# Graph attention, layers 1 to 3: exponential factors in the table rows in place of raw scores

## The chip, the core and the metric

The program runs on one core of one Trainium2 chip. The metric is the device time of a run in microseconds (us); the time before is the median of three runs, 3008.34 us (2991.2 to 3010.58). Five engines of the core do the work: TensorE (PE, whose weight loads the profile lists as PEld), VectorE (DVE), ScalarE (ACT), GpSimd (POOL) and SyncE (SP). Each runs its own instructions in order; semaphores tie them to each other, and DMA queues move data between the device's memory (DRAM) and the two memories on chip, SBUF and PSUM.

## The reference

Four graph-attention layers work on one graph of 3327 nodes and on features x (3327 x 512, float32). Each layer normalises x, applies ReLU, lets each node average over its neighbours with attention weights, and adds the result to x. The heads are 8, 4, 1 and 8; layers 0 and 1 count a node as its own neighbour, and layers 1 and 2 apply ELU.

```python
def layer(x, l):                                  # l = 0 .. 3, H = 8, 4, 1, 8
    h = relu(layernorm(x))
    v = (h @ W[l]).reshape(n, H, 512 // H)
    s = einsum("nhd,hd->nh", v, a_own[l])         # score of the node that averages
    d = einsum("nhd,hd->nh", v, a_other[l])       # score of the neighbour
    e = leaky_relu(s[:, None, :] + d[None, :, :], 0.2)
    e = where(neighbours[:, :, None], e, -inf)
    alpha = softmax(e, axis=1)
    y = einsum("ijh,jhd->ihd", alpha, v).reshape(n, 512)
    return x + (elu(y) if l in (1, 2) else y)
```

A neighbour's weight before the division by the sum is exp(leaky(s + d)), with leaky(z) = max(z, 0.2 z). Since the exponential of a sum is a product, it is also exp(0.2 s) exp(0.2 d) max(exp(0.8 s) exp(0.8 d), 1). The first factor depends only on the node that averages, so the division by the sum of the weights removes it.

## The kernel before

**Prologue.** The nodes are padded to 3328, 26 tiles of 128. The first 313 us read the adjacency matrix, take from each row a list of its neighbours' numbers, sort the rows by the length of their lists (CAPS holds the longest list of each tile, 36 down to 11) and project the features for layer 0 into a table in DRAM. Only then does `tile_gat_lists` begin, which all that follows is about.

**The table.** Between layers, each node's row lies in a DRAM table (`tabs`, two of them in turn). A row has ROW = 528 numbers in two halves of 264: 256 projected features and 8 score columns. Behind the first half are the node's own scores s, behind the second its scores d as a neighbour. Layer 0 has a table of its own (`tabx`).

**A tile with lists (class Tile).** A step is a group of four list entries of one tile: 133 steps in layer 0, then 118, 72 and 105. `fetch` is called seven steps ahead: POOL issues one indirect DMA for each entry (L834), which brings 128 table rows, one for each partition, into g; in layers 1 to 3 the node's own row (entry 0) comes through SP (L865). `scored` runs one step ahead of the products. It copies s out of the own row at a tile's first step (L885), adds s to the d columns of g (z, L887), applies the leaky slope (L889), both on VectorE, and lets ACT write the exponential into pw (L890). pw is a PSUM bank that holds the weights of a whole tile; in layer 2 it lies in SBUF instead. `group` then multiplies the gathered features by the weights on VectorE (m, L918, four operations of 512 columns; a tile's first goes to the accumulator itself), and PE adds m to the accumulator ("bank") with an identity as the weights (L923). Buffers: seven g, three m, two accumulators. In layer 2, with its one head, VectorE accumulates by itself (L909, L911).

**Behind a tile.** `finish` and `ends` spread the rest over the next steps: the sum of the weights and its reciprocal (L929 to L931), the division (L937, L941), ELU with two ACT operations (neg L947, ex L949) and one on VectorE (L955), the sum into x (L957, L961), the centred row xn and its squares on ACT (L969, L972), the reciprocal root on VectorE (ve L977, then L434 to L440), the transposes (L450), the ReLU (hT, L457), the projection for the next layer (L468), the scaling by ACT into v (L475), and SP's write of v to the table (L995). In PSUM, the projection's result pv has a bank for each half of the row.

**Tiles done densely.** The tiles with the longest lists go against all 3328 rows under a mask: one tile in layer 1, nine in layer 2, three in layer 3 (DENSE = [0, 1, 9, 3]). Layers 1 and 3 use `Several`: 52 units u, the 26 tiles of rows twice, half of the heads each time. For a unit SP loads half of the table rows and a mask (L1250, L1251; three buffers each). In the first 26 units ACT makes exp(0.8 d) and exp(0.2 d) of all heads (L1261, L1262). Then ACT forms r = relu(exp(0.8 s) exp(0.8 d) - 1) for each head (L1267) and the features times exp(0.2 d) (L1278, L1279; two buffers); VectorE masks r + 1 (L1283), PE multiplies (L1301, into "whole"). exp(0.8 s) of the dense tiles, one node for each column, is made once (L1241, L1243). `Wholes` does the same for layer 2, three passes of three tiles over 26 row tiles j: the loads of ve and the mask (L1105, L1107; four and three buffers), in the first pass exp(d), exp(0.2 d) and its negative (L1115 to L1117), r (L1119), the mask (em, L1126), the products (L1153), and partial sums of the weights on POOL and VectorE.

**The order.** The order of PE, VectorE, ACT and POOL is written out by hand. `later(step, place, piece)` files a piece under a step and one of three places, and a loop issues each step as: fetches, the "first" pieces, `scored` of the next step, the "scored" pieces, `group` of this step, the "last" pieces. The dense work's masked tile and product are "first" pieces, and its r, features and next loads "scored" pieces. So they stand in the engines' queues between the pieces of the list tiles:

```python
do("first")
if s + 1 < len(steps):
    steps[s + 1][0].scored(steps[s + 1][1])
do("scored")
if 0 <= s < len(steps):
    tl, i = steps[s]
    tl.group(i)
    if i == len(tl.k0) - 1:
        tl.finish(s)
do("last")
```

The waits follow from the buffers that instructions share; in this program a wait that concerns a PSUM buffer covers its whole bank.

Of the kernel before, what the change touches and what calls it, by code (L numbers as in the profile page):

```python
# [18 lines left out]
P = 128  # L19
# [504 lines left out]
def tile_gat_stack(ctx: ExitStack, tc: tile.TileContext, x, adj, adjT, ws, avs, out):  # L524
# [32 lines left out]
    spare = late.tile([P, 2, slots.parts[1].columns], F32, name="spare")  # L557


    with ExitStack() as c1:  # L560
# [49 lines left out]
        def late_constants():  # L610
# [5 lines left out]
            for t in tabs:  # L616
                nc.sync.dma_start(t[NP:NP + 1, :], pad[:, :ROW])
# [173 lines left out]
    with cond.Else():  # L791
        tile_gat_lists(tc, x, adj, ws, avs, out, ident, half, slots, L, low, spare, tabx, tabs)
# [3 lines left out]
def tile_gat_lists(ctx: ExitStack, tc: tile.TileContext, x, adj, ws, avs, out, ident, half, slots, L, low, spare, tabx, tabs):  # L796
# [48 lines left out]
    class Tile:  # L845
# [29 lines left out]
        def scored(self, i):  # L875
# [4 lines left out]
            if i == 0:  # L880
                self.po = pools["o"].tile([P, BANK], F32, name="bank")
                pw = next(scores)
                K = CAPS[t]
                self.wt, self.s = pw[:, :K * 8].rearrange("p (k h) -> p k h", h=8), pw[:, K * 8:K * 8 + H]
                nc.vector.tensor_copy(self.s, g[:, n, F:F + H] if self.l == 0 else g[:, 0, F // 2:F // 2 + H])  # L885
# [5 lines left out]
            if self.l == 0:  # L891
                ranks = n - (i == 0)
                nc.scalar.activation(slots(t, max(k0, 1), count=ranks), g[:, :ranks, F // 2], AF.Copy)
                if i == 0:
                    nc.scalar.activation(xs[self.t], g[:, n, :F], AF.Copy)

# [95 lines left out]
        def rows(self):  # L992
            if self.W is not None:
                v = scaled(nc, self.pv, self.rstd, work)
                nc.sync.dma_start(tabs[(self.l + 1) % 2][self.t * P:(self.t + 1) * P, :], v)  # L995
# [86 lines left out]
    class Wholes:  # L1082


        def __init__(self, l, W):
            self.l, self.tiles = l, [Whole(l, t, W) for t in range(ND)]
            self.s = pools["e"].tile([P, ND], F32, name="s", bufs=1)
            for t in range(ND):
                nc.sync.dma_start(self.s[:, t:t + 1], tabs[l % 2][t * P:(t + 1) * P, F // 2:F // 2 + 1])
            self.b, self.c, self.mc = [pools["e"].tile([P, NT], F32, name=n, bufs=1) for n in ("b", "c", "mc")]  # L1090
# [4 lines left out]
        def targets(self, p):  # L1095

            pa = pools["t"].tile([P, F // P, P], F32, name="pt")
            for q in range(3):
                nc.tensor.matmul(pa[:, q, :], self.s[:, 3 * p + q:3 * p + q + 1].to_broadcast([P, P]), ident,
                                 start=True, stop=True)  # L1100
            nc.scalar.activation(self.a[p], pa[:, :3, :], AF.Exp, scale=1.0 - SLOPE)
# [7 lines left out]
        def weights(self, p, j):  # L1109
            if p == ND // 3:  # L1110
                return
            b, c, mc = [t[:, j:j + 1] for t in (self.b, self.c, self.mc)]
            if p == 0:
                d = self.v[p, j][:, ROW - 8:ROW - 7]
                nc.scalar.activation(b, d, AF.Exp)  # L1115
                nc.scalar.activation(c, d, AF.Exp, scale=SLOPE)
# [4 lines left out]
        def masked(self, p, j):  # L1121
# [4 lines left out]
            nc.vector.scalar_tensor_tensor(self.e[p, j], self.r.pop((p, j)), self.c[:, j:j + 1],  # L1126
# [43 lines left out]
        def place(self, n):  # L1170

            per = n // (ND // 3)
            for p in range(ND // 3):
                s0 = p * per
                later(s0 - 4 if p else -1, "first", lambda p=p: self.targets(p))
                for j in range(NT):
                    s = s0 + j * (per - 2) // NT
                    later(max(s - 3, -1), "first", lambda p=p, j=j: self.load(p, j))
# [27 lines left out]
    class Several:  # L1206
# [3 lines left out]
        def __init__(self, l, n, W):  # L1210
# [10 lines left out]
            self.c, self.b = [room(NT * Q * 2).rearrange("p (j h) -> p j h", j=NT) for _ in range(2)]  # L1221

# [3 lines left out]
            self.s = room(n * 8).rearrange("p (t h) -> p t h", h=8)  # L1226
            for t in range(n):
                nc.sync.dma_start(self.s[:, t, :self.H],
                                  tabs[l % 2][t * P:(t + 1) * P, F // 2:F // 2 + self.H])
            self.per = BANK // DV - (self.H == 8)  # L1230

        def begin(self):
# [20 lines left out]
        def weights(self, u):  # L1253
# [215 lines left out]
```

## Time and profile before

The profiled execution spanned 2971.7 us.

| | us |
|---|---|
| median of three runs | 3008.34 |
| the three runs | 3008.34, 2991.2, 3010.58 |
| span of the profiled execution | 2971.7 |
| PE busy (share of the span) | 2211.9 (74%) |
| DVE busy | 1923.1 (65%) |
| POOL busy | 1731.4 (58%) |
| ACT busy | 934.6 (31%) |

The table says that no engine is busy throughout. The page's costliest groups of instructions name the work: each line gives the source line, engine, operation, output and inputs with their shapes and the count; then busy time and the mean ns of one; then the engine's idle time just before them, and what ended most of it.

```profile
L923 PE MATMUL bank<-m,ident 128*128 128x512 f32 x2414 | 1232.2, 659 | 335.9 <-DVE m L918 197.3
L918 DVE TENSOR_TENSOR m<-g,pw 128x512 f32<-128x512 f32 x1207 | 752.5, 682 | 384.1 <-ACT pw L890 209.2
L890 ACT ACTIVATE pw<-z 128x32 f32<-128x32 f32 (+4 forms) x356 | 67.8, 191 | 850.7 <-DVE z L889 484.2
```

The three are the chain of one step read backwards: PE adds m, VectorE makes m from g and the weights, ACT makes the weights. The last column is the reading to learn: before the multiplications VectorE had stood idle for 384.1 us in all, of which 209.2 us ended when ACT delivered pw; and ACT's own work there takes 191 ns each time. A wait of this kind need not mean that the exponential is slow. ACT may have come to it late because its queue held something else. The same column is given for a single instruction in the chronological lists below, in brackets at the end of a line.

### The profile page before, as it was taken

The numbers are of one execution on the slowest core, as the hardware profiler recorded it, in microseconds if no ns is written. First come the engines' busy times: TensorE is split into PE (matmuls) and PEld (weight loads), VectorE is DVE, ScalarE is ACT, GpSimd is POOL, SyncE is SP. The second block draws the span as 40 slices with busy tenths as digits, with TensorE's granted clock in tenths as the row PEclk, the third lists the DMA queues.
The fourth block names the chain that finished last, engine by engine and source line by source line (L and its number), as shares of the span: only waits on it lengthen the run. The fifth ranks groups of instructions, "written<-read, shape, count | busy, mean of one in ns | idle before, by whom it ended". The sixth has DMA issues, their size and how long they took to land.

```text
span 2971.7 us, 27155 instructions
## 1 busy us (share of the span) xinstructions
PE 2211.9 (74%) x7082; PEld 1246.1 (42%) x7082; DVE 1923.1 (65%) x4968; ACT 934.6 (31%) x2502; POOL 1731.4 (58%) x1717
## 2 busy tenths in 40 slices
PE   4777677776777764767777877588696688878887
PEld 2564233343433332434444444244354454545443
DVE  7987666655565533656665665598888366666665
ACT  5872122322221111322222322244333333323330
POOL 7885455565566635544556562676664556555653
PEclk9988888888898887988888898799898898989888
DMA  6885576786676756755667673787785566656663
GB/s 230 325 291 161 165 228 200 211 254 207 195 225 197 199 130 200 200 157 174 187 190 210 179 209 92 234 255 240 241 246 153 168 193 204 185 170 198 195 189 111
DMA packets 260731, 594.21 MB, mean 200 GB/s; under 512 B 103699, under 2 KB 121107, under 8 KB 256214
## 3 DMA queue, kind: packets, MB, share of 16 engines
q0 software_dynamic: 124368, 432.13, 49.8%
q1 hardware_dynamic: 132454, 153.45, 16.4%
q10 hardware_dynamic: 3744, 6.82, 0.7%
q8 instruction: 57, 0.93, 0.1%
q14 instruction: 108, 0.88, 0.1%
HBM read 542.60 MB, written 49.65 MB: 199 GB/s over the span
## 4 chain that ended last, share of the span: by engine, by line
PE 24%; DVE 18%; issue 14%; another core or an unknown queue 8%; ACT 5%; POOL 3%; DMA 2%; SPq 0%; DVEq 0%; POOLq 0%; ACTq 0%
PE bank L923 16%; DVE m L918 6%; PE pv L468 4%; PE whole L1301 3%; DVE bank L911 3%; POOL g L834 3%; ACT r L1267 1%; DVE z L889 1%; DVE z L887 1%; DVE x L961 1%; PE whole L1153 1%; DMA g<-tab,idxb 1%; DVE em L1126 1%; DVE q L438 1%
## 5 line engine op out<-in xcount | busy, mean ns | idle before, releaser
L923 PE MATMUL bank<-m,ident 128*128 128x512 f32 x2414 | 1232.2, 659 | 335.9 <-DVE m L918 197.3
L918 DVE TENSOR_TENSOR m<-g,pw 128x512 f32<-128x512 f32 x1207 | 752.5, 682 | 384.1 <-ACT pw L890 209.2
L834 POOL DMA_INDIRECT g<-tab,idxb x712 | 678.8, 953 | 482.0 <-issue 197.1
L923 PEld LDWEIGHTS bank<-m,ident 128*128 128x128 f32 x2414 | 488.8, 211 | 942.1 <-issue 582.4
L468 PE MATMUL pv<-w,hT 128*128 128x264 f32 x1664 | 434.9, 416 | 87.8 <-ACT hT L457 61.8
L834 POOL DMA_INDIRECT g<-tabx,twiceb x342 | 324.8, 950 | 230.7 <-issue 147.7
L834 POOL DMA_INDIRECT g<-tab,idxa x297 | 283.7, 955 | 248.4 <-issue 83.9
L468 PEld LDWEIGHTS pv<-w,hT 128*128 128x128 f32 x1664 | 334.1, 205 | 190.3 <-ACT hT L457 68.7
L890 ACT ACTIVATE pw<-z 128x32 f32<-128x32 f32 (+4 forms) x356 | 67.8, 191 | 850.7 <-DVE z L889 484.2
L1153 PE MATMUL whole<-ve,em 128*128 128x512 f32 x468 | 229.4, 642 | 54.1 <-issue 22.9
L1301 PE MATMUL whole<-L,room 128*128 128x130 f32 x1248 | 173.3, 290 | 59.9 <-issue 59.5
L1301 PEld LDWEIGHTS whole<-L,room 128*128 128x128 f32 x1248 | 164.7, 202 | 91.4 <-issue 89.7
L694 POOL TENSOR_TENSOR key<-a,keys 128x3328 int32<-128x3328 int32 (+1 forms) x29 | 189.3, 6530 | 16.3 <-DVE cand L703 11.8
L911 DVE SCALAR_TENSOR_TENSOR bank<-g,L,bank 128x512 f32<-128x512 f32 x243 | 183.3, 754 | 11.1 <-remote 2.0
L1153 PEld LDWEIGHTS whole<-ve,em 128*128 128x128 f32 x468 | 94.0, 206 | 167.4 <-issue 124.5
L834 POOL DMA_INDIRECT g<-tabx,twicea x99 | 94.7, 956 | 104.1 <-issue 51.1
L450 PE MATMUL pt<-ident,xn 128*128 128x128 f32 x416 | 70.8, 298 | 104.7 <-ACT xn L969 60.8
L703 DVE MAX8 cand<-key 128x8 f32<-128x208 int32 x416 | 144.3, 365 | 0.1
L475 ACT ACTIVATE v<-pv,rstd 128x528 f32<-128x528 f32 x78 | 54.2, 694 | 274.4 <-remote 126.5
L1267 ACT ACTIVATE r<-low,L 128x384 f32<-128x384 f32 x208 | 121.2, 583 | 16.9 <-remote 9.5
L918 DVE TENSOR_TENSOR bank<-g,pw 128x512 f32<-128x512 f32 x74 | 51.5, 696 | 100.7 <-ACT pw L890 69.2
L450 PEld LDWEIGHTS pt<-ident,xn 128*128 128x128 f32 x416 | 54.7, 153 | 144.4 <-ACT xn L969 69.1
(180 smaller groups left out, 2195.7 us busy)
## 6 DMA issues: line engine op xcount, KB each, us to landing
a<-in_adj SPq DMA_DIRECT2D x25, 1664.0 KB
tab<-v SPq DMA_DIRECT2D x78, 264.0 KB
ve<-tab SPq DMA_DIRECT2D x78, 264.0 KB
g<-tab SPq DMA_DIRECT2D x65, 264.0 KB
tabx<-vx SPq DMA_DIRECT2D x26, 528.0 KB
g<-tab,idxb POOLq DMA_INDIRECT x712
low<-tab SPq DMA_DIRECT2D x52, 132.0 KB
spare<-tab SPq DMA_DIRECT2D x52, 132.0 KB
```

Source lines behind the costliest of these rows:

```text
L450: nc.tensor.transpose(pt[:, k, :], xn[:, k * P:(k + 1) * P], ident)
L468: nc.tensor.matmul(pv[:, s, :HF + 8], hT[:, k, :], W.w[:, k, s, :], start=(k == 0), stop=(k == KC - 1))
L694: nc.gpsimd.tensor_tensor(key[:, c:c + quarter], a[:, c:c + quarter], keys[:, c:c + quarter], OP.mult)
L703: nc.vector.max(cand[:, g * 8:(g + 1) * 8], key[:, g * SEG:(g + 1) * SEG])
L834: nc.gpsimd.indirect_dma_start(out=out_, out_offset=None, in_=table, in_offset=bass.IndirectOffsetOnAxis(ap=which, axis=0))
L890: nc.scalar.activation(self.wt[:, k0:k0 + n, :H], z, AF.Exp)
L911: nc.vector.scalar_tensor_tensor(acc, v, w, acc, OP.mult, OP.add)
L918: nc.vector.tensor_tensor(out_.rearrange("p (s h d) -> p s h d", s=2, d=D), v.rearrange("p s (h d) -> p s h d", d=D), wt[:, k0 + q, :H].re ...
L923: nc.tensor.matmul(self.po, ident, m[:, q, :], start=False, stop=(k0 + q == K - 1), skip_group_check=True)
L1153: nc.tensor.matmul(tl.po.rearrange("p (s m) -> p s m", s=2), e[:, q * P:(q + 1) * P], v.rearrange("p (s m) -> p s m", s=2)[:, :, :F // 2], ...
L1267: nc.scalar.activation(self.r[:, h, :], self.a[:, g, :], AF.Relu, bias=-1.0, scale=self.b[:, j, g:g + 1])
L1301: nc.tensor.matmul(dst, e[:, h, q * P:(q + 1) * P], mov, start=False, stop=(j == NT - 1), skip_group_check=True)
```

## The change

In layers 1 to 3 the table rows carry exponentials of the scores, and the weights come from products and maxima on VectorE.

- `rows` adds four small ACT operations per tile, between the scaling (L475) and the table write (L995): a copy of d, scaled, out of pv; exp(0.8 s) into a tile `mine` that stays in SBUF, one column per tile and head; and two exponentials of d, which take the place of raw scores in v. With several heads these are exp(0.8 d) and exp(0.2 d), half of the heads behind each half of the row; with one head exp(d) and exp(0.2 d).
- `scored` of layers 1 to 3 calls `factored` and ends there: with several heads z = exp(0.8 s) exp(0.8 d), then max(z, 1) exp(0.2 d) straight into pw; with one head a single operation. The copy of s, the addition, the leaky slope and ACT's exponential leave these layers. Layer 0 keeps them.
- The dense parts no longer load s nor make exponentials of d; they read the factors from the rows loaded for the products. The exponential that made exp(0.8 s) for the targets becomes a copy.
- In layer 2 the first row tile of the second and third pass is loaded a step earlier.
- The tables' padding row becomes zeros. `mine` is handed through as an argument (not shown).

```diff
--- before
+++ after
@@ -555,6 +555,7 @@
...
     spare = late.tile([P, 2, slots.parts[1].columns], F32, name="spare")
+    mine = [late.tile([P, NT, n], F32, name=f"mine{n}") for n in (1, 8)]
...
@@ -614,7 +615,7 @@
...
             for t in tabs:
-                nc.sync.dma_start(t[NP:NP + 1, :], pad[:, :ROW])
+                nc.sync.dma_start(t[NP:NP + 1, :], pad[:, ROW:])
...
@@ -882,7 +883,11 @@
...
                 self.wt, self.s = pw[:, :K * 8].rearrange("p (k h) -> p k h", h=8), pw[:, K * 8:K * 8 + H]
-                nc.vector.tensor_copy(self.s, g[:, n, F:F + H] if self.l == 0 else g[:, 0, F // 2:F // 2 + H])
+                if self.l == 0:
+                    nc.vector.tensor_copy(self.s, g[:, n, F:F + H])
+            if self.l > 0:
+                self.factored(g, k0, n)
+                return
             z = small.tile([P, GROUP, 8], F32, name="z")[:, :n, :H]
...
@@ -893,6 +898,23 @@
...
                     nc.scalar.activation(xs[self.t], g[:, n, :F], AF.Copy)
+        def factored(self, g, k0, n):
+            H = HEADS[self.l]
+            a = mine[self.l % 2][:, self.t, :H]
+            w = self.wt[:, k0:k0 + n, :H]
+            if H == 1:
+                c0 = ROW - 8
+                nc.vector.scalar_tensor_tensor(w, g[:, :n, c0:c0 + 1], a, g[:, :n, c0 + 1:c0 + 2], OP.mult, OP.max)
+                return
+            Q, c0 = H // 2, F // 2
+            rows = g[:, :n, :].rearrange("p k (s m) -> p k s m", s=2)
+            z = small.tile([P, GROUP, 8], F32, name="z")[:, :n, :H].rearrange("p k (s h) -> p k s h", s=2)
+            nc.vector.tensor_tensor(z, rows[:, :, :, c0:c0 + Q],
+                                    a.rearrange("p (s h) -> p s h", s=2).unsqueeze(1).to_broadcast([P, n, 2, Q]), OP.mult)
+            nc.vector.scalar_tensor_tensor(w.rearrange("p k (s h) -> p k s h", s=2), z, 1.0,
+                                           rows[:, :, :, c0 + Q:c0 + 2 * Q], OP.max, OP.mult)
         def group(self, i):
...
@@ -992,6 +1014,19 @@
         def rows(self):
...
                 v = scaled(nc, self.pv, self.rstd, work)
+                H = HEADS[self.l + 1]
+                d = small.tile([P, 8], F32, name="d")[:, :H]
+                nc.scalar.activation(d, self.pv[:, 1, F // 2:F // 2 + H], AF.Copy, scale=self.rstd)
+                nc.scalar.activation(mine[(self.l + 1) % 2][:, self.t, :H], v[:, F // 2:F // 2 + H], AF.Exp,
+                                     scale=1.0 - SLOPE)
+                if H == 1:
+                    parts = [v[:, ROW - 8 + i:ROW - 7 + i] for i in range(2)]
+                else:
+                    Q, d = H // 2, d.rearrange("p (s h) -> p s h", s=2)
+                    halves = v.rearrange("p (s m) -> p s m", s=2)
+                    parts = [halves[:, :, F // 2 + i * Q:F // 2 + (i + 1) * Q] for i in range(2)]
+                nc.scalar.activation(parts[0], d, AF.Exp, scale=1.0 if H == 1 else 1.0 - SLOPE)
+                nc.scalar.activation(parts[1], d, AF.Exp, scale=SLOPE)
                 nc.sync.dma_start(tabs[(self.l + 1) % 2][self.t * P:(self.t + 1) * P, :], v)
         def ends(self, s):
...
@@ -1084,10 +1119,7 @@
         def __init__(self, l, W):
             self.l, self.tiles = l, [Whole(l, t, W) for t in range(ND)]
-            self.s = pools["e"].tile([P, ND], F32, name="s", bufs=1)
-            for t in range(ND):
-                nc.sync.dma_start(self.s[:, t:t + 1], tabs[l % 2][t * P:(t + 1) * P, F // 2:F // 2 + 1])
-            self.b, self.c, self.mc = [pools["e"].tile([P, NT], F32, name=n, bufs=1) for n in ("b", "c", "mc")]
+            self.mc = pools["e"].tile([P, NT], F32, name="mc", bufs=1)
...
@@ -1096,9 +1128,9 @@
...
             for q in range(3):
-                nc.tensor.matmul(pa[:, q, :], self.s[:, 3 * p + q:3 * p + q + 1].to_broadcast([P, P]), ident,
+                nc.tensor.matmul(pa[:, q, :], mine[self.l % 2][:, 3 * p + q, 0:1].to_broadcast([P, P]), ident,
                                  start=True, stop=True)
-            nc.scalar.activation(self.a[p], pa[:, :3, :], AF.Exp, scale=1.0 - SLOPE)
+            nc.scalar.activation(self.a[p], pa[:, :3, :], AF.Copy)
         def load(self, p, j):
...
@@ -1109,11 +1141,9 @@
         def weights(self, p, j):
...
                 return
-            b, c, mc = [t[:, j:j + 1] for t in (self.b, self.c, self.mc)]
+            b, c = [self.v[p, j][:, ROW - 8 + i:ROW - 7 + i] for i in range(2)]
+            mc = self.mc[:, j:j + 1]
             if p == 0:
-                d = self.v[p, j][:, ROW - 8:ROW - 7]
-                nc.scalar.activation(b, d, AF.Exp)
-                nc.scalar.activation(c, d, AF.Exp, scale=SLOPE)
                 nc.scalar.activation(mc, c, AF.Copy, scale=-1.0)
...
@@ -1123,7 +1153,7 @@
...
             self.e[p, j] = self.two[:, j % 2, :]
-            nc.vector.scalar_tensor_tensor(self.e[p, j], self.r.pop((p, j)), self.c[:, j:j + 1],
+            nc.vector.scalar_tensor_tensor(self.e[p, j], self.r.pop((p, j)), self.v[p, j][:, ROW - 7:ROW - 6],
                                            self.mk.pop((p, j)), OP.add, OP.mult)
...
@@ -1175,7 +1205,8 @@
...
                     s = s0 + j * (per - 2) // NT
-                    later(max(s - 3, -1), "first", lambda p=p, j=j: self.load(p, j))
+                    early = s0 - 4 if p and j == 0 else s - 3
+                    later(max(early, -1), "first", lambda p=p, j=j: self.load(p, j))
...
@@ -1218,15 +1249,9 @@
...
             self.e = [room(Q * n * P).rearrange("p (h c) -> p h c", h=Q) for _ in range(2)]
-            self.c, self.b = [room(NT * Q * 2).rearrange("p (j h) -> p j h", j=NT) for _ in range(2)]
             self.vs = [room((Q + (self.H == 8)) * DV) for _ in range(2)]
...
             self.mk = [room(n * P // 4).bitcast(U8) for _ in range(3)]
-            self.s = room(n * 8).rearrange("p (t h) -> p t h", h=8)
-            for t in range(n):
-                nc.sync.dma_start(self.s[:, t, :self.H],
-                                  tabs[l % 2][t * P:(t + 1) * P, F // 2:F // 2 + self.H])
             self.per = BANK // DV - (self.H == 8)
         def begin(self):
...
@@ -1238,9 +1263,9 @@
...
                     for h in range(4):
-                        nc.tensor.matmul(pa[:, h, :], self.s[:, q, h0 + h:h0 + h + 1].to_broadcast([P, P]), ident,
-                                         start=True, stop=True)
-                    nc.scalar.activation(self.a[:, h0:h0 + 4, q * P:(q + 1) * P], pa, AF.Exp, scale=1.0 - SLOPE)
+                        nc.tensor.matmul(pa[:, h, :], mine[self.l % 2][:, q, h0 + h:h0 + h + 1].to_broadcast([P, P]),
+                                         ident, start=True, stop=True)
+                    nc.scalar.activation(self.a[:, h0:h0 + 4, q * P:(q + 1) * P], pa, AF.Copy)
         def load(self, u):
...
@@ -1256,16 +1281,13 @@
...
             n, Q, H, D = self.n * P, self.Q, self.H, self.D
-            if i == 0:
-                d = self.v[u % 3][:, ROW // 2 - 8:ROW // 2 - 8 + H]
-                nc.scalar.activation(self.b[:, j, :], d, AF.Exp, scale=1.0 - SLOPE)
-                nc.scalar.activation(self.c[:, j, :], d, AF.Exp, scale=SLOPE)
+            b = self.v[u % 3][:, F // 2:F // 2 + Q]
             r = pools["r"].tile([P, self.n, BANK], F32, name="r").rearrange("p a b -> p (a b)")
...
                 nc.scalar.activation(self.r[:, h, :], self.a[:, g, :], AF.Relu, bias=-1.0,
-                                     scale=self.b[:, j, g:g + 1])
+                                     scale=b[:, h:h + 1])
         def features(self, u):
...
@@ -1273,7 +1295,7 @@
...
             vs = self.vs[u % 2].rearrange("p (h d) -> p h d", d=self.DV)
-            c = self.c[:, j, (1 - i) * Q:(2 - i) * Q]
+            c = self.v[u % 3][:, F // 2 + Q:F // 2 + 2 * Q]
             for h in range(Q):
```

More of the change, by code (lines that the diff above doesn't have):

```diff
@@ L791, in tile_gat_stack, with tile_gat_lists @@
     with cond.Else():
-        tile_gat_lists(tc, x, adj, ws, avs, out, ident, half, slots, L, low, spare, tabx, tabs)
+        tile_gat_lists(tc, x, adj, ws, avs, out, ident, half, slots, L, low, spare, mine, tabx, tabs)
 @with_exitstack
-def tile_gat_lists(ctx: ExitStack, tc: tile.TileContext, x, adj, ws, avs, out, ident, half, slots, L, low, spare, tabx, tabs):
+def tile_gat_lists(ctx: ExitStack, tc: tile.TileContext, x, adj, ws, avs, out, ident, half, slots, L, low, spare, mine, tabx, tabs):
     nc = tc.nc
```

## The prediction

> **What bounds it now.** First the head of the page, then busy time by stage. I cut the span at the last table write of each layer: layer 0 is 313 to 1112 us, layer 1 to 1845, layer 2 to 2310, layer 3 to the end.
>
> ```profile
> span 2971.7 us, 27155 instructions
> ```
>
> Columns: busy us (instructions) of PE, PEld, DVE, ACT, POOL; granted PE clock; DMA share; GB/s.
>
> ```profile
> 313.00:1112.00 799.00, 580.32 (x1642) 293.51 (x1643) 456.45 (x1209) 176.55 (x468) 455.33 (x479) 0.87 0.69 203
> 1112.00:1845.00 733.00, 548.15 (x1542) 289.66 (x1541) 445.94 (x1199) 202.02 (x613) 385.12 (x406) 0.86 0.63 181
> 1845.00:2310.00 465.00, 354.46 (x1040) 201.26 (x1038) 365.17 (x734) 171.00 (x414) 291.24 (x308) 0.88 0.73 221
> 2310.00:2971.70 661.70, 525.58 (x2028) 311.17 (x2028) 410.10 (x801) 204.72 (x634) 367.57 (x386) 0.89 0.63 181
> ```
>
> No engine fills layers 1 and 3: PE comes nearest (75% and 79%). In layer 2 VectorE and PE are level. So the question is who waits for whom. VectorE's waits, layer 1, then layer 3 (us in total, times, longest):
>
> ```profile
> DVE ve L977 <- ACT waste L972: 60.5, 15, 11.3
> DVE bank L955 <- ACT ex L949: 43.1, 7, 13.1
> DVE m L918 <- ACT pw L890: 36.4, 51, 10.8
> DVE bank L955 <- issue: 32.6, 9, 7.9
> ```
>
> ```profile
> DVE m L918 <- ACT pw L890: 98.8, 41, 10.9
> DVE m L918 <- issue: 26.8, 29, 8.4
> DVE bank L918 <- ACT pw L890: 22.4, 13, 9.0
> ```
>
> The waits on the exponential (pw, L890), with the products' "issue" rows, which I count to it, are 98.8 + 26.8 + 22.4 + 6.4 (bank, issue) = 154.4 us in layer 3. In layer 1 they are 36.4 + 15.7 + 7.8 + 2.4 = 62.3, but there 136.2 us (first, second and fourth row) are on two other results of ACT. PE's waits, layer 1, then layer 3:
>
> ```profile
> PE bank L923 <- DVE m L918: 97.6, 23, 10.3
> PE bank L923 <- issue: 52.3, 15, 15.3
> ```
>
> ```profile
> PE whole L1301 <- issue: 59.5, 56, 2.6
> PE bank L923 <- issue: 35.8, 25, 10.9
> PE bank L923 <- DVE m L918: 27.1, 19, 9.7
> ```
>
> So VectorE's lateness costs PE 62.9 us in layer 3, and 149.9 in layer 1. One stall of layer 1 in order of time, ACT, then VectorE:
>
> ```profile
> 1355.37 0.40 ACT L1278 ACTIVATE low<-low 128x128 f32<-128x128 f32 x1 [8.95 <-remote]
> ```
>
> ```profile
> 1345.52 1.88 DVE L918 TENSOR_TENSOR m<-g,pw 128x512 f32<-128x512 f32 x3 [0.25 <-ACT pw L890]
> 1358.71 0.15 DVE L977 TENSOR_SCALAR ve<-squares 128x1 f32<-128x1 f32 x1 [11.31 <-ACT waste L972]
> ```
>
> ACT stands at L1278, whose buffer PE's dense products (L1301) must have read; all that ACT owes VectorE waits behind it. VectorE's next wait here is the squares, not pw: this stall the change leaves. In layer 3 it is pw (a product at 2666.19 had waited 10.66 us for it).
>
> ```profile
> 1355.00:1360.00 5.00, 1.12 (x4) 0.72 (x4) 1.13 (x6) 2.93 (x7) 0.00 (x0) 0.54 0.33 113
> 1360.00:1365.00 5.00, 1.70 (x2) 0.84 (x3) 4.52 (x15) 0.70 (x2) 0.29 (x1) 0.50 0.00 0
> ```
>
> After it PE's clock is 0.50: a stall costs its idle time and slow matmuls.
>
> **Layer 3 (105 groups).** Out of the loop go 105 exponentials on ACT (191 ns) and VectorE's hand-over to them. The 154.4 us of waits don't become time saved: PE is next. At full clock a bank matmul record follows the last by 0.43 us and a dense one by 0.11 (the timeline's steady stretches), so PE needs 720 x 0.43 + 1248 x 0.11 + some 13 for the rest = 460 us; it is busy 525.6, the difference being the slow clock, and idle 62.9 behind VectorE. Bounds: 0 and 62.9 + 65.6 = 128. VectorE may now run on through ACT's stalls until a masked tile (L1283) lacks its r or three m buffers are full; at 410 us over 105 steps (3.9 us each) that is over 8 us, the length of most stalls. I take two thirds of the idle time (42) and a fifth of the clock's share (13): **-55**.
>
> [...]
>
> **Layer 1 (118 groups).** Half of the 62.3 us of waits, since the 136.2 us on squares and ex stay where they are: -31 (bounds 0 and, with PE's idle time halved, -75). Against it stand the new row factors: four small ACT operations between v (L475) and the table write, just ahead of xn and squares, on which VectorE waits. L1261 to L1262 starts 0.10 us later, a small operation takes 0.19: two that wait for their forerunner and two that don't make some 0.55 us a tile, 25 tiles: +14. **-17.**
>
> The weights' own price on VectorE: the copy of s goes (25 x 0.15, in layer 3 22 x 0.165: -7.4), two operations stay two. The new multiply reads SBUF alone; the add it replaces read PSUM too (164 ns in layer 1, 178 in layer 3). The SBUF-only add of layer 2 took 241, so the multiply may cost 118 x 0.077 + 105 x 0.063 = +15.7, or nothing more. I take +8, and 0 in the sum: VectorE waits longer than that in both layers; without that cover it is +8 whole. [...]
>
> **Layer 2 (72 groups).** Three operations and an ACT hop become one on VectorE:
>
> ```profile
> L887 DVE TENSOR_TENSOR z<-g,L 128x4 f32<-128x4 f32 (+3 forms) x72 | 17.4, 241 | 18.0 <-DMA g<-tab,idxa 16.8 <-issue 0.5
> L889 DVE SCALAR_TENSOR_TENSOR z<-z 128x4 f32<-128x4 f32 (+3 forms) x72 | 14.9, 207 | 4.8 <-issue 2.3
> ```
>
> L889's kind stays; L887 (17.4) and the copy (17 x 0.144 = 2.5) go. VectorE is busy 112.6 of 131 us in the middle pass, so most of 19.9 is time: -18. New waits: in passes 2 and 3 ACT's r (L1119) now needs ve itself, which only the products needed. SP issues it late, behind L1107 and full buffers (80.4 us on L1153). In pass 1, where ACT already needs it, L1115 started 2.8 to 5.2 us after late issues. Laid over the issues of passes 2 and 3, r would be late 12 to 23 times (22 to 66 us of ACT), and VectorE's masked tile behind it 3 to 15 us; queued behind r on ACT are ex and squares. I take +6. The first tile of a pass is loaded a step earlier: one ve and one mk on SP, 0.32 us each, ahead of that step's g and tab transfers, 0. **-12.**
>
> **Layer 0 and the borders.** The same 0.55 us for 26 tiles, half of it under idle time of ACT: **+7** (0 to 14). In layer 2 ACT is idle 292 us and hides it. The last tile of three layers carries it in full: **+2**. The 13 loads of s go, with PE's 5.0 and ACT's 8.0 us at layer 1's start; VectorE waits 16.0 us there for the first gathers anyway (16.8, 16.3 later): 0.
>
> Sum: -55 - 17 - 12 + 7 + 2 = -75. The span becomes 2896.7; the median of the runs is 36.6 above the profiled span, so **2933 us**.
>
> **Rivals.** (1) More is recovered (0.16): layer 3 near its bound of 128, layer 1 near 60: about -150, 2858. For it: PE waits 212.8 us in both for VectorE. Against: squares and ex. (2) The wait only changes its name (0.15): ACT held by PE is not cured, so r, squares or full m buffers hold VectorE instead. Left are the short hand-overs and layer 2, -20: 2988. (3) ve's lateness passes whole to layer 2 (0.06): up to +55, -20 left, 2988. (4) Slower (0.13): VectorE frees g sooner, and POOL's gathers run on without the pauses in which PE's word now reaches ACT (released as POOL had stopped and DMA fell from 0.77 to 0.33). ACT waits 182.7 us for PE in layer 1 and 114.6 in layer 3 ("remote" included); if these grow by over 75/297, a quarter, the sign turns; by a half, +149 - 75 = +74, 3082. That the weights stay on ACT is excluded: in the built program the products of layers 1 to 3 wait for VectorE and PE alone.
>
> **The numbers.** The forecast (-45 to -120) has 0.50. About 1%, 30 us, is what a measurement can tell from no change: faster 0.50 + 0.16 = 0.66, same 0.15 + 0.06 = 0.21, slower 0.13. The range goes from 2845, which takes in most of (1), to 3035, which takes in (2) and (3) with unknown costs against them; it leaves out most of (4) and an edge of (1).
>
> **What would show it.** No wait of m on pw in layers 1 to 3; layer 3's PE idle time before L923 near 20, its window near 605; layer 1's ve and ex rows unchanged or longer; VectorE in layer 2 busy some 20 less; waits of r on ve's DMA in passes 2 and 3. It is wrong if layer 3 doesn't shrink, if m's waits on PE grow by what pw's lose, or if ACT's waits on PE lengthen.

## The result, and the profile after

The change made the kernel slower: 3032.9 us against 3005.6 (medians of 14 runs each), a ratio of 1.0099, interval 1.0078 to 1.0121. The forecast was 2933. On other chips, where the kernel before takes 2430 us, the same change made it faster, 0.9943 (0.9923 to 0.9962). Why the layers that were to gain gave nothing on the first chip is worked out below; what makes that chip's loss is open.

First a correction to the working. The profiled execution of before spanned 2971.7 us and all 14 runs of that kernel lie between 2991 and 3026; the profiled run of after took 3038.0 us at a span of 3036.2. So some 2 us lie around a span, not 36.6: the first profile caught an execution shorter than any run shown. The profiles differ by 64.5 us, the medians by 27.3, and a stage's difference between these two is to be read with that in mind.

Stages of after, from POOL's first gather on, cut where SP issues the last table write of a layer; columns as in the prediction:

```profile
273.10:1133.20 860.10, 612.09 (x1696) 303.97 (x1695) 473.24 (x1259) 192.01 (x574) 476.04 (x502) 0.84 0.67 197
1133.20:1892.80 759.60, 553.74 (x1557) 294.07 (x1556) 445.24 (x1177) 193.75 (x547) 384.11 (x406) 0.85 0.60 175
1892.80:2364.60 471.80, 355.67 (x1023) 198.46 (x1023) 353.46 (x641) 169.32 (x394) 290.33 (x308) 0.88 0.71 218
2364.60:3036.20 671.60, 531.16 (x2028) 316.17 (x2026) 408.00 (x779) 189.10 (x477) 366.57 (x386) 0.87 0.61 178
```

By the same cuts before had 838.7, 739.4, 458.9 and 661.0 us (the prediction began layer 0 at 313 us, though the gathers begin at 273.7, and ended layer 1 some 7 us early). Every layer grew: by 21, 20, 13 and 11. Layer 0's weights are untouched; it has only the new row factors.

What VectorE waits for, in layer 1 of after, then in layer 3 (us in total, times, longest). L977 is L955 of before, L999 is L977, L963 is L941, L1305 is L1283, L1300 is L1278; the first two lines of the second list are of before:

```profile
DVE bank L977 <- ACT ex L971: 111.7, 10, 16.5
DVE ve L999 <- ACT waste L994: 65.1, 13, 12.3
DVE bank L977 <- issue: 24.9, 3, 8.5
...
DVE ve L999 <- issue: 8.9, 4, 5.7
```

```profile
DVE room L1283 <- issue: 19.0, 2, 10.6
DVE bank L941 <- remote: 6.7, 2, 3.3
...
DVE room L1305 <- issue: 96.7, 14, 10.8
DVE room L1305 <- remote: 30.6, 2, 21.7
DVE bank L963 <- remote: 27.2, 3, 10.6
...
DVE bank L963 <- PE whole L1323: 16.3, 2, 13.8
...
DVE room L1305 <- PE bank L945: 10.5, 1, 10.5
DVE bank L963 <- issue: 9.6, 1, 9.6
```

No wait on pw is left in layers 1 to 3. But in layer 1 the rows on ex and squares, which stood at 136.2 us, are 210.6: they took 74 us more where pw gave up 62. In layer 3, where pw gave up 154, the masked dense tile now waits 137.8 us (21.8 before, with two short rows on ACT) and the division of a finished accumulator 57.5 (with the row on PE's bank, 4.4; before 9.2). VectorE's time not busy went from 251 to 264 us there. What PE waits for in layer 3 of after:

```profile
PE whole L1323 <- issue: 85.9, 78, 2.5
PE bank L945 <- issue: 35.1, 27, 8.7
PE bank L945 <- DVE m L940: 7.2, 5, 2.6
```

The list tiles did give back some time (62.9 us of waits before, 42.3 now), and the dense products took it (59.5, now 85.9).

The lists call most of the masked tile's waits "issue", with no releaser, but the trace of after has more. The tile needs r from ACT, a mask from SP, and a buffer that PE's products two units earlier have read. Of the 137.8 us, 128.3 passed after r and those products had both ended. In 15 of the 17 waits an event of PE's semaphore stands within 0.1 us of the moment when VectorE goes on, and in 15 ACT's features (L1300) had been let go at most 0.2 us before. At 2474.95 us, for example, ACT goes on after 18.47 us of waiting and at 2475.14 VectorE after 9.82; r had ended 18.7 us and the products 21.1 us earlier. So VectorE now stands where ACT stands: at the message of PE's semaphore that its work is done, called PE's word below, which comes long after the work.

### The profile page after: what moved, and what is told of

It is laid out like the page before. It is cut to its first block, busy times and chain, and to the rows that moved or that the text cites. A ratio compares the mean times of both kernels' runs of the same rounds, so it can differ in the third digit from the quotient of the medians.

```text
span 3036.2 us, 26902 instructions
## 1 busy us (share of the span) xinstructions
PE 2227.6 (73%) x7082; PEld 1254.0 (41%) x7082; DVE 1908.9 (63%) x4831; ACT 923.1 (30%) x2363; POOL 1727.2 (57%) x1717
## 4 chain that ended last, share of the span: by engine, by line
PE 28%; DVE 14%; issue 12%; another core or an unknown queue 11%; ACT 4%; DMA 3%; POOL 2%; SPq 1%; DVEq 0%; POOLq 0%; ACTq 0%
PE bank L945 17%; DVE m L940 5%; PE whole L1323 5%; PE pv L468 4%; DVE bank L933 2%; PE whole L1183 2%; POOL g L835 2%; DMA ve<-tab 1%; ACT v L475 1%; DMA g<-tab,idxb 1%; DVE x L983 1%; DMA g<-tab,idxa 0%; DVE q L438 0%; DVE pw L916 0%
## 5 line engine op out<-in xcount | busy, mean ns | idle before, releaser
L1323 PE MATMUL whole<-L,room 128*128 128x130 f32 x1248 | 176.7, 290 | 86.1 <-issue 85.9
L475 ACT ACTIVATE v<-pv,rstd 128x528 f32<-128x528 f32 x78 | 54.2, 694 | 410.8 <-remote 271.2
L963 DVE TENSOR_TENSOR bank<-bank,den 128x512 f32<-128x512 f32 x74 | 51.3, 694 | 123.6 <-remote 72.0
L1305 DVE SCALAR_TENSOR_TENSOR room<-r,low 128x1536 f32<-128x1536 f32 x35 | 61.3, 1752 | 99.1 <-issue 79.7
L1289 ACT ACTIVATE r<-low,spare 128x384 f32<-128x384 f32 x136 | 79.5, 585 | 95.0 <-DVE room L1305 62.1
```

Source lines behind the costliest of these rows:

```text
L475: nc.scalar.activation(v.rearrange("p (s n) -> p s n", s=2), pv[:, :, :ROW // 2], AF.Copy, scale=rstd)
L1289: nc.scalar.activation(self.r[:, h, :], self.a[:, g, :], AF.Relu, bias=-1.0, scale=b[:, h:h + 1])
L1323: nc.tensor.matmul(dst, e[:, h, q * P:(q + 1) * P], mov, start=False, stop=(j == NT - 1), skip_group_check=True)
```

## The experiments

Four explanations were put to the test. **R**: the four ACT operations of the row factors hold back the table write, xn and squares. **G**, the prediction's fourth rival: VectorE runs ahead, the gathers run on, and PE's word reaches ACT later. **N**, the second rival: the wait only changes its name; **N2** is its sharper form, that VectorE itself must wait for PE's word. **V**: in layer 2 ACT's r waits for ve.

The experiments ran on five chips. On four of them the kernel before takes 2430 us; on the fifth, which had one experiment, it takes 2991. Ratios are to the kernel before on the same chip.

**The parts, one at a time.** The row factors alone, on the kernel before (four operations of the same shapes, results unused):

```diff
                 v = scaled(nc, self.pv, self.rstd, work)
...
+                d = small.tile([P, 8], F32, name="d")[:, :H]
+                nc.scalar.activation(d, self.pv[:, 1, F // 2:F // 2 + H], AF.Copy, scale=self.rstd)
+                nc.scalar.activation(mine[(self.l + 1) % 2][:, self.t, :H], v[:, F // 2:F // 2 + H], AF.Exp,
+                                     scale=1.0 - SLOPE)
+                for _ in range(2):
+                    nc.scalar.activation(v[:, ROW - 8:ROW - 8 + H], d, AF.Copy)
```

> The kernel before, with four small ACT operations per tile of the shapes of the change put between the scaling into v and the table write in layers 0, 1 and 2; their results are not used (two of them write the values that v already holds). Theory R (row factors: the four operations hold back the table write, xn and the squares on ACT): 15 to 35 us slower than before, layer 0 and layer 1 longer by some 10 us each, layer 3 unchanged. Theory G (VectorE runs ahead, gathers run on without pauses, PE's word reaches ACT later): within 8 us of before. Theory N (all parts near nothing, the waits change their names): within 8 us.

Then the change for one layer alone; everything that the change does asks whether the layer is in a set, here for layer 1 (where layer 2 keeps its old form, its b and c lie in a free buffer):

```diff
+FACT = {1}
...
-            if self.l > 0:
+            if self.l in FACT:
                 self.factored(g, k0, n)
                 return
```

> The change made for layer 1 alone (its factors are made at the end of layer 0; layers 2 and 3 as before; layer 3 has a table of its own, because the two kinds of rows need different padding). Theory R: 10 to 15 us slower, all of it in layer 0 (the four operations are there), layer 1 no longer than before. Theory G: 10 to 20 us slower, in layer 1, with ACT's waits on PE there longer than before, layer 0 unchanged. Theory N: within 8 us.

> The change made for layer 2 alone (factors made at the end of layer 1). Theory R: 5 to 15 us slower, in layer 1; layer 2 itself shorter or equal. Theory G: within 8 us, since layer 2's products wait little for ACT. A third theory, V (ACT's r now waits for ve in passes 2 and 3): layer 2 longer by 5 to 20 us and its wait of VectorE's masked tile on ACT longer, layer 1 unchanged.

> The change made for layer 3 alone (factors made at the end of layer 2, where ACT is idle most). Theory R: faster by 5 to 40 us, in layer 3, as predicted for that layer. Theory G: 5 to 20 us slower, in layer 3, with ACT's waits on PE there longer. Theory N: within 8 us, the waits on pw replaced by waits on r, on full m buffers and on the accumulator.

And the changed kernel itself where the parts had run:

> The changed kernel itself. The parts ran where the kernel before took 2429 us, not 3005, and where PE's semaphores hardly fell silent while it worked (7 stretches of over 5 us with more than 20 matmuls in them, 51 us in all, against 62 stretches and 676 us in the first profile). If the chip is of that kind: the parts add up to -18 - 2 + 4 = -16 us, so 0.990 to 0.997 of before. If it takes some 3005 us before: 1.008 to 1.012 as measured first. Theory G says that the loss belongs to the chip that is slow; theory R, that it is the same number of us on both (some +27).

| kernel | ratio | interval | us against before |
|---|---|---|---|
| row factors alone | 1.0037 | 1.0024 to 1.0051 | +10 |
| layer 1 alone | 0.9930 | 0.9917 to 0.9944 | -18 |
| layer 2 alone | 0.9991 | 0.9979 to 1.0002 | -2 |
| layer 3 alone | 1.0022 | 1.0011 to 1.0033 | +4 |
| whole change | 0.9943 | 0.9923 to 0.9962 | -14 |

On these chips the parts add up (-16 against -14), and the profiles show where. Layer 1 goes from 559.9 us to 542.8 by its weights, and the row factors of the next layer add 5 to its old form (565.1); with the whole change it takes 545.7. Layer 2 goes from 447.4 to 439.3, and the row factors add 3 to 5 to its old form. Its new form bears them worse: with the whole change it takes 454.5, where layers 1 and 2 alone (the last experiments below) leave it at 443.6 (one profile each). Layer 0 takes none (646.2, with the row factors 646.7). R had expected 15 to 35 us for the row factors, G a loss in layers 1 and 3, V a longer layer 2, and N nothing anywhere (at most 8): none of them holds as it stands, and the loss of the first chip isn't there. Layer 3 shows N plainly. VectorE's waits in layer 3 with the weights of before (from the kernel with layer 1 alone), then with the new ones (layer 3 alone):

```profile
DVE m L944 <- ACT pw L899: 39.5, 79, 3.9
...
DVE bank L944 <- ACT pw L899: 12.6, 23, 1.9
```

```profile
DVE z L918 <- DMA g<-tab,idxb: 40.4, 32, 3.7
DVE z L918 <- DMA g<-tab,idxa: 18.3, 4, 16.8
```

Here 52.1 us on pw went, and the waits on the gathers rose from 16.5 us to 58.7: the layer takes 497.6 us in place of 498.6, with PE busy 467.8 of them.

**A cheaper row.** Three operations that don't wait for each other in place of four in a chain, the one for mine behind the write; for layers 1 and 2, and for all three. One more small operation per tile, on VectorE or POOL, makes the scales (rs, not shown):

```diff
-                nc.scalar.activation(d, self.pv[:, 1, F // 2:F // 2 + H], AF.Copy, scale=self.rstd)
...
-                nc.scalar.activation(parts[1], d, AF.Exp, scale=SLOPE)
-                nc.sync.dma_start(tabs[(self.l + 1) % 2][self.t * P:(self.t + 1) * P, :], v)
+                nc.scalar.activation(parts[1], d, AF.Exp, scale=self.rs[:, 1:2])
+                nc.sync.dma_start(tabs[TAB[self.l + 1]][self.t * P:(self.t + 1) * P, :], v)
+                nc.scalar.activation(mine[(self.l + 1) % 2][:, self.t, :H], self.pv[:, 0, F // 2:F // 2 + H], AF.Exp,
+                                     scale=self.rs[:, 0:1])
```

> The change for layers 1 and 2 alone, and in the rows three ACT operations that read the projection and do not wait for each other, in place of four in a chain; the one that fills mine comes behind the table write; one small VectorE or POOL operation per tile makes 0.8 and 0.2 times the reciprocal root. On a chip with 2429 us before: 20 to 30 us faster than before (18 + 2 from the parts, and some 5 of the row factors' 9). On one with 3005: theory R says 5 to 25 us better than the changed kernel; theory G says layer 3 as before, layer 1 as slow as in the changed kernel.

> The whole change, with three independent ACT operations in the rows in place of four in a chain, the one for mine behind the table write. On a chip with 2430 us before: 4 to 10 us better than the changed kernel's 0.9943, so 0.990 to 0.993, if the row factors' 9 us come from the four operations ahead of the write. On one with 3005: theory R says 10 to 25 us faster than the changed kernel, theory G the same as it within 8 us.

Measured: 0.9935 (0.9922 to 0.9948) and 0.9975 (0.9962 to 0.9988). The first gained 16 us where 20 to 30 had been expected. The second should have beaten the whole change and did not, so fewer operations ahead of the write don't by themselves make the row cheaper; this variant also has the operation for rs and reads pv three times. Why it is no better was not found.

**Imitating the first chip.** What differs there? In the first profile ACT waits 182.7 us for PE in layer 1 and 114.6 in layer 3; on the other chips, with before's weights, the 114.6 are 6.9. PE's words arrive late. Where v (L475) had to wait in layers 0 and 1, it started 5.8 us on average after the end of the projection's last matmul (32 places, at most 17.0); with the whole change on the other chips it was 0.04 (27 places). The events thin out as well: 2023 of PE's instructions raise its semaphore, and the first trace has 1664 such events. In 62 stretches of over 5 us (676 us in all) more than 20 matmuls start and no event comes; on the other chips 5 to 7 stretches, some 50 us. In the stall that the prediction shows, ACT was let go when the gathers had stopped. So ACT was made to wait for the gathers where it waits for PE, ahead of the scaling into v and of each unit's features:

```diff
+    def drain():
+        nc.scalar.activation(small.tile([P, 1], F32, name="drain", bufs=1), newest[0], AF.Copy)
...
             self.groups.append((k0, n, g))
+            newest[:] = [g[:, n - 1, 0:1]]
...
+                drain()
                 v = scaled(nc, self.pv, self.rstd, work)
```

> The kernel before, with one small ACT operation ahead of each scaling into v (layers 0 to 2) and of each unit's features (layers 1 and 3); it reads the table rows gathered last, so ACT goes on only when the gathers issued so far have landed. That imitates, where PE's word comes at once, what the first profile showed: ACT released when the gathers had drained. Expected on a chip with 2430 us before: 100 to 600 us slower, with stages nearer to those of the first profile (layer 1 739, layer 3 661 us), VectorE waiting for pw in layers 1 and 3. On a chip with 3005: little change, under 60 us, since ACT is released late there anyway.

> The changed kernel with the same small operation in the same places (and two buffers in place of four for the copy of d). Theory G (where ACT is released only as the gathers drain, VectorE's freedom lengthens ACT's waits and takes the gain): 0 to 60 us slower than the coupled kernel before. If G is wrong, and the loss on the first chip has another cause: faster than the coupled kernel before by 14 us or more, since VectorE no longer waits for pw.

Then VectorE too, ahead of each group's products, against the group five steps ahead (the last but one that `newest` now holds):

```diff
+            nc.vector.tensor_copy(small.tile([P, 1], F32, name="held", bufs=1), newest[-1])
             m = pools["m"].tile([P, GROUP, F], F32, name="m")
```

> The coupled kernel before, and VectorE too goes on with a group (layers 0, 1 and 3) only when the gathers of the group five steps ahead have landed, by a small copy from their rows ahead of the group's products. On the first chip PE's word was late for every engine that waits for PE, so for VectorE's m and accumulators as well as for ACT; the first coupling held ACT alone. On a chip with 2430 us before: 2950 to 3400 us.

> The changed kernel with both couplings. Theory N2 (on the first chip VectorE would have waited for PE's word itself, so that its wait on pw covered a wait that comes anyway): within 30 us of the kernel before with both couplings, where the coupling of ACT alone left a gain of 146 us. If the gain is still over 60 us, VectorE's own waits for PE's word do not explain the first chip, and its loss stays open.

And against the last group fetched, six ahead ("tight"), also with the row factors alone:

> The kernel before with ACT coupled as in the first pair, and VectorE coupled to the group six steps ahead, the one fetched last, in place of five. 3000 to 3700 us, where the kernel before takes 2430.

> The changed kernel with the same tight coupling. Theory N2 + R (where VectorE waits for the drained gathers anyway, layers 1 and 3 gain nothing, and what is left is the price of the row factors and of layer 2): 5 to 40 us slower than the tight kernel before; layers 1 and 3 within 8 us of it, layers 0 and 2 longer by 5 to 15 us each. Without N2: faster by 30 us or more.

> The tight kernel before with the four small ACT operations per tile in the rows of layers 0 to 2, their results unused. Theory R: 10 to 35 us slower than the tight kernel before, half of it or more in layer 0, against 9 us without couplings (where layer 0 took none of it). If it is within 8 us, the row factors are not what is left on the first chip.

| kernel, on chips with 2430 us before | us | layer 0 | layer 1 | layer 2 | layer 3 |
|---|---|---|---|---|---|
| ACT held, before | 2910.4 | 722.0 | 785.5 | 504.1 | 621.2 |
| ACT held, after | 2764.7 | 734.0 | 721.9 | 509.6 | 516.9 |
| both held, before | 2942.4 | 748.3 | 785.9 | 504.6 | 625.9 |
| both held, after | 2912.1 | 756.3 | 772.0 | 515.6 | 589.4 |
| tight, before | 4024.7 | 1068.0 | 1162.4 | 504.5 | 1018.8 |
| tight, after | 4034.4 | 1066.9 | 1166.1 | 516.2 | 1016.9 |
| tight, row factors alone | 4037.4 | 1069.9 | 1160.2 | 516.2 | 1013.5 |

With ACT alone held late, the change gains 146 us, 104 of them in layer 3. So G is not what the imitation shows: ACT let go late makes the change better, since VectorE no longer stands behind ACT (in layer 3, 167.1 us of waits on pw before, none after). With VectorE held too, 30 are left, at the edge of what N2 had forecast: layer 3 still gains 37 and layer 1 14, layers 0 and 2 lose 8 and 11. With the tight hold it loses 10 (no run of the one overlaps the other's, though the intervals of the ratios, 1.651 to 1.658 and 1.656 to 1.663, overlap a little), and the row factors alone lose 13. In the tight pair layers 0, 1 and 3, where VectorE is held, change by -1, +4 and -2 us; layer 2 takes 12 more with the change, and 12 more with the row factors alone. R's forecast that half or more would lie in layer 0 failed (+2). VectorE's waits in layer 3, both held, before and then after:

```profile
DVE held L918 <- DMA g<-tab,idxb: 72.1, 44, 3.4
DVE m L924 <- ACT pw L895: 48.8, 65, 1.2
DVE held L918 <- DMA g<-tab,idxa: 36.1, 15, 15.1
...
DVE bank L924 <- ACT pw L895: 13.9, 17, 1.2
```

```profile
DVE held L940 <- DMA g<-tab,idxb: 99.0, 57, 3.9
DVE held L940 <- DMA g<-tab,idxa: 46.9, 17, 16.4
```

The 62.7 us on pw went; the hold took 37.7 of them. That is N2 where the hold puts the second wait in by hand: the wait on pw covered another that was running at the same time.

The looser hold with the row factors alone was to give their price there:

> The kernel before with both couplings of the looser kind (2942 us) and the four small ACT operations per tile in the rows of layers 0 to 2, their results unused. Theory R: 10 to 30 us slower than 2942, mostly in layers 0 and 2, so that without the row factors the change would have gained 40 to 60 us there and not 30. Within 8 us: the row factors cost nothing where the time is nearest to that of the first chip, and what made the loss there stays open.

This run was on the fifth chip (before 2991.1), where the held kernel before did not run: 3106.0 us, 1.0382 (1.0349 to 1.0416), so the price stays open. But its profile tests what the hold imitates. ACT's waits in layer 1:

```profile
ACT drain L846 <- DMA g<-tab,idxb: 195.4, 46, 6.9
...
ACT drain L846 <- DMA g<-tab,idxa: 77.8, 14, 21.8
...
ACT v L478 <- PE pv L471: 14.6, 2, 9.2
```

ACT waits 273 us for gathers, and then PE's word is there: 14.6 us are left of the 182.7 on PE for v and the features, and the silent stretches of that layer fall from 20 (213 us) to 6 (48 us). In layer 3 the features' waits on PE fall likewise, from 114.6 us to 14.3. Layer 0 doesn't follow: v still waits 89.7 us there in 8 places behind the hold, and the silent stretches are 14 (171 us), where the first profile had 9 (120 us). So the hold is like the first chip in layers 1 and 3, as far as ACT's waits go. That the gathers delay PE's word isn't shown: in layer 1 ACT stood longer for them (273 us) than it had for PE (183), and a late word may have come in the meantime.

**The rest.** Layers 1 and 2 with the change as it is, and two of the parts again:

> The change for layers 1 and 2 alone, with the four operations in a chain as in the change. On a chip with 2430 us before: 20 to 30 us faster than before (0.988 to 0.992), since layer 3's part gained 1 us in layer 3 and cost 3 to 15 in the rows of layer 2. On one with 3005: 0 to 20 us slower than before.

> The kernel before with the four small ACT operations in the rows of layers 0 to 2, unused, once more: the last call ran where the kernel before takes 2991 us, as in the first measurement. On such a chip theory R says 15 to 35 us slower than before; within 8 us, the loss of 27 us is not that of the row factors. On the other kind (2430 us): 9 us slower, as before.

> The change made for layer 3 alone, once more. On a chip with some 3000 us before: the prediction's step says 55 us faster (less what the row factors cost in layer 2); theory N2 says within 15 us of before, the waits on pw replaced by waits on PE and on ACT's r. On the other kind: 5 us slower, as before.

The first gave 0.9926 (0.9910 to 0.9942), 19 us faster than before where 20 to 30 had been expected: as good as layer 1 alone, and not clearly better than the whole change. The other two ran on the quicker kind again, with 1.0039 (1.0024 to 1.0054) and 1.0011 (0.9999 to 1.0023).

## Why the prediction was wrong

**The step that failed** is layer 3's: "I take two thirds of the idle time (42) and a fifth of the clock's share (13): -55". It took VectorE to be free of ACT once pw is gone, with "a masked tile (L1283) lacks its r or three m buffers are full" as a distant limit. VectorE did stop at the masked tile, but neither for r nor for m: it waited for PE's late word itself, as ACT does. The wait on pw had covered that wait. In the place of 154.4 us on pw stand 137.8 on the masked tile, 128.3 of them after its inputs had ended, and 57.5 on finished accumulators. The layer came out 11 us longer in the first chip's profiles and 1 us shorter on the other chips; it was 104 shorter where ACT alone was held late, 37 where VectorE was held too, and 2 in the tight hold. This is the second rival, which had 0.15, though it named r, squares and m buffers as the next limit. Its price of -20 has no term for the row factors, which alone cost 10 us on the quicker chips.

**Layer 1**, -17, failed in the same way on the first chip (+20): squares and ex were said to "stay where they are", and they grew by more than pw gave up. Where PE's word comes at once the sum came out, 559.9 to 545.7 with the whole change, but by luck: the weights gave 17 where 31 was taken, and the row factors took 3 to 5 where 14 was.

**The row factors** were sized at 0.55 us a tile, and that was right: the four take 257, 204, 206 and 189 ns in the profile after, but they overlap, and the last ends 0.58 us behind v (median). What such a delay costs was not. Layer 2 did not hide them for ACT being idle: 447.4 us became 450.6 on the other chips (with its new form 443.6 became 454.5), 504.5 became 516.2 in the tight hold. In layer 0 the forecast was +7; the first chip shows +21, the other chips nothing, the two looser holds 12 and 8, the tight one -1. Layer 0 has no other edit, so its growth on the first chip is theirs or chance; no run on such a chip parts the two.

**Layer 2.** Two sizes were off. VectorE's single operation was priced like the one it resembles (207 ns) and takes 332, so VectorE is busy 11 us less, not 20. And r's waits on ve, forecast as 22 to 66 us of ACT in 12 to 23 places, are there; that size was right:

```profile
ACT r L1149 <- DMA ve<-tab: 55.3, 16, 6.7
```

But VectorE's masked tile behind them went from 26.4 us of waits to 48.2, 22 more, where 3 to 15 had been named and 6 taken. V holds on the first chip, where the layer is 13 us longer in the profiles; with layer 2 alone on the others, the layer still gains 8.

**VectorE's price of the weights** was put at up to +15.7, with +8 taken as hidden. The SBUF-only multiply takes 172 ns in layer 1 against 166 for the add with its PSUM operand, and 183 against 182 in layer 3: next to nothing. The 241 ns of layer 2's SBUF-only add show in neither layer.

**The fourth rival** named the right sign, by a mechanism that the runs don't bear out in layer 3 and leave open in layer 1. Its test, ACT's waits on PE in layers 1 and 3, went from 297.3 to 542.5 us, 82% more, where a quarter was to turn the sign and a half to cost 74 us. But ACT's time not busy in the two layers grew by 54 only (537.1 to 565.9 and 457.0 to 482.5): ACT no longer waits for VectorE's scores, so it stands at the same late word earlier. A longer wait isn't a later release. The two profiles show the release itself: in layer 3, where ACT's features waited, they started 7.9 us on average after the products that had to free their buffer (20 units), in after 6.0 (28 units). For v the mean went from 5.3 to 6.7 us in layer 1, but also from 6.1 to 9.8 in layer 0, where VectorE's part is the old one. PE's silent stretches went from 62 (676 us) to 57 (652 us).

What stays open: why the first chip loses 27 us where the imitation with the nearest time (2942) still gains 30. That layer 3 gained nothing there is N2, as the trace of after shows; in layer 1 the waits moved on to squares and ex. The tight hold reaches the sign, with N2 in layers 1 and 3 and R in layer 2; on the first chip itself the parts were not measured.

## What to carry to other kernels

Before a wait is priced, ask what else its engine would have waited for at that moment; a wait can cover others, and taking it away then gives back less than it took (in layer 3, 52.1 us of waits on pw went and the layer became 1 us shorter on the quicker chips; with both engines held, 62.7 and 37). To learn that, hold each engine artificially and see which hold eats the gain. And measure on more than one chip before a gain or loss of 1% is taken for the kernel's.

## What the runs showed of the hardware that was not expected

The same program took 2430 us on four chips and 2991 on a fifth (first measurement: 3006), with the gathers' POOL instructions at 947 (row factors alone) and 949 ns (first profile; medians). What differs in the traces is how late PE's word comes: 5.8 us on average for v in layers 0 and 1 against 0.04. Two other words are not late in the first profile: VectorE's z reaches ACT's pw 0.04 us after its end, and ACT's squares reach VectorE's ve after 0.03 (medians where the wait was for them). The granted clock differs as well (0.873 over the first profile, 0.947 with layer 1 alone), but it fell to 0.887 on a quicker chip when ACT was held, so a lower clock can follow from the waits. In the one run where ACT waited first for the gathers in flight, on such a chip, it then hardly waited for PE's word in layers 1 and 3 (14.6 and 14.3 us for v and the features), but still did in layer 0 (89.7 us). What makes PE's word late on the slower chip, no run here shows.
